# A recurrence in 32 chunks of 32 steps instead of 64 of 16, and an output written in pieces of 2 KB

## The chip, the cores and the metric

The kernel runs on one core of one Trainium2 chip. The metric is the device time of one execution in microseconds (us), taken as the median of several runs; the profile is that of one further execution. A core has a matrix engine (PE, with weight loads listed apart as PEld), a vector engine (DVE), an activation engine (ACT), GpSimd (POOL), SyncE (SP), which here only issues transfers, and 16 DMA engines that all queues share.

## The reference, cut to what matters

Two layers work on x of 8 batches, 1024 tokens (64 by 16) and 128 channels, all float32. Layer 0 is an 8-head attention with two softmaxes and a feed-forward part. Layer 1 adds an additive (tanh) attention and then a recurrent part, and only what follows the recurrent part's input projection is touched here:

```python
Wx = jnp.einsum('bti,hi->bth', x, W)                    # x: layer-normed tokens, 8 x 1024 x 128
Wx = (Wx - mean) * rsqrt(var + 1e-5) * gamma + beta      # mean, var over all 8*1024 tokens
def step(yt, wx_t):
    yt = sigmoid(wx_t + yt @ V.T)
    return (yt, yt)
_, ys = jax.lax.scan(step, zeros, Wx over t)             # 1024 steps, 8 batches side by side
out = t + ys                                             # t: the residual stream
```

The scan has 1024 dependent steps for each batch. V is an orthogonal matrix and the sigmoid's slope is at most a quarter, so that the influence of a state dies away fast: a state that was started from zero some 16 steps too early is, to float32 precision for this purpose, the right one. Both kernels use that.

## The kernel before, in words

The body is `fast_path`. Nearly all of its time is a planned part: `plan.add` collects the operations of both layers for all batches with estimated costs and priorities, and `plan.emit` writes them out in an order of its own. During it, the finished residual stream of each batch goes out to a DRAM buffer `parked[b]` (line 1201, in two transfers of 256 KB), the projected inputs go to `parked_wx[b]`, and near the end they come back into `wx`.

After `main.close()` (line 1318) a straight, hand-ordered stage follows, and this is what the change touches:

- The statistics become a scale `sc` and an offset `off` (lines 1323 to 1330).
- `xr`, the residual stream of all batches, is fetched from `parked` (line 1336, eight transfers of 512 KB).
- DVE writes `ws`, the scaled inputs, one position l of all chunks at a time (line 1342, sixteen instructions of 512 columns).
- The recurrence. The 1024 tokens are cut into NCH = 64 chunks of LCH = 16 steps. All chunks of all batches, 64 x 8 = 512 columns, take one step together. Each chunk first runs through the 16 inputs of the chunk ahead of it (`early`), starting from nothing, and then through its own 16: 32 dependent steps. The 512 columns are two halves of 256 (chunks 0 to 31 and 32 to 63), which take turns. For each half of each step PE adds `ws` through an identity matrix (line 1361) and `V y` (line 1363) in one PSUM bank `acc`, ACT takes the sigmoid into `y` (line 1365), and in the second 16 steps DVE copies `y` to its place in `ys` (line 1370). Float32 matmuls run as two passes each in the trace, so a half step is four passes. The first chunk of a batch has no chunk ahead of it: it is skipped in the early steps, and its state is set to zero by a memset (line 1368).
- The output. For every batch and every four blocks of 128 tokens, PE transposes four blocks of `ys` into a PSUM tile `yt` (line 1378; two tiles), DVE adds `xr` into `ot` (line 1380; three tiles), and a transfer, issued in turn by ACT and SP, writes `ot` to `out` (line 1382). A partition of `ot` holds four tokens that lie 128 tokens apart, so each contiguous piece in DRAM is one token, 512 bytes.

Instructions on one engine run in program order; an engine waits for another only where data or a buffer asks for it.

Of the kernel before, what the change touches and what calls it, by code (L numbers as in the profile page):

```python
# [560 lines left out]
def fast_path(ctx: ExitStack, tc: tile.TileContext, a: dict, fits):  # L561
# [5 lines left out]
    nc = tc.nc  # L567
    NB, N, C = a["x"].shape
    H = a["wqn"].shape[1]
    NT = N // P  # L570
# [1 line left out]
    G = 16  # L572
    M = N // G
    SCALE = 1.0 / math.sqrt(C)
    NCH = 64
    LCH = N // NCH
    NX = 2
    NE = 2
# [3 lines left out]
    dram = ctx.enter_context(tc.tile_pool(name="dram", bufs=1, space=bass.MemoryType.DRAM))  # L582
# [4 lines left out]
    def tile_of(pool, name, shape):  # L587
        return pool.tile(shape, F32, tag=name, name=name)
# [6 lines left out]
    wx = tile_of(keep, "wx", [P, NB, N])  # L595
    parked_wx = [tile_of(dram, f"parked_wx{b}", [P, N]) for b in range(NB - 1)]
    wx_stats = tile_of(keep, "wx_stats", [P, NB, 2, 6])

    parked = [tile_of(dram, f"parked{b}", [P, NT, C]) for b in range(NB)]

    def load(pool, name, shape, eng):
        t = pool.tile(shape, F32, tag=name, name=name + "_sb")
        eng.dma_start(out=t, in_=a[name])
        return t
# [48 lines left out]
    vf_sb = load(const, "vf", [P, C], nc.sync)  # L653
# [8 lines left out]
    ident = tile_of(const, "ident", [P, P])  # L662
# [10 lines left out]
    half = tile_of(const, "half", [P, P])  # L673
# [81 lines left out]
    def through_bank(pe, weight, r, evict, where, more, w, pri, choice=two):  # L755

        bank = Bank(*choice)
        n = len(plan.ops)
        add(("PE", weight), lambda _: pe(bank()), r=r, w=[("bank", n)], pri=pri, take=bank, wait=more + w)
        add(where, lambda e: evict(e, bank()), r=[("bank", n)] + more, w=w, pri=pri, give=bank)  # L760

    def transposes(srcs):
        def fn(bank):
            for i, s in enumerate(srcs):
                nc.tensor.transpose(bank[:, i * P : (i + 1) * P], s, ident)  # L765

        return fn

    def copy(dst):
        def fn(e, bank):  # L770
            src = bank
            if len(dst.shape) == 3:
                src = bank[:, : dst.shape[1] * P].rearrange("p (t c) -> p t c", c=P)
            if e == "ACT":
                nc.scalar.activation(dst, src, AF.Copy)
            else:
                nc.vector.tensor_copy(dst, src)  # L777

        return fn
# [306 lines left out]
    def layer1(b):  # L1086
# [27 lines left out]
        for pair in order:  # L1114
# [48 lines left out]
            for it in range(NT):  # L1163
                if it not in attended and done.issuperset(range(it + 1)):
                    attended.add(it)
                    attention(b, it, X, kX, B, kB, E_at, L1)

    def attention(b, it, X, kX, B, kB, E_at, L1):

        for j0 in range(it + 1, NT, 4):  # L1170
            js = range(j0, min(j0 + 4, NT))
            through_bank(
                transposes([E_sb[:, E_at[it] + j - it, :] for j in js]), 0.08 + 0.12 * len(js),
                [("E", it, j) for j in js],
                copy(ET[:, j0 - 1 : j0 - 1 + len(js), :]), ("DVE", 0.15 + 0.135 * len(js)), [],
                [("ET", j) for j in js], L1,
            )

        def attend(bank):
            for j in range(NT):  # L1180
                lhsT = E_sb[:, E_at[j] + it - j, :] if j <= it else ET[:, j - 1, :]
                nc.tensor.matmul(bank[:, : C + 1], lhsT, B[:, j, :], start=j == 0, stop=j == NT - 1)
# [13 lines left out]
        if it % 4 != 3:  # L1196
            return
        qh = it // 4
        Xg = X[:, 4 * qh : 4 * qh + 4, :]
        add(  # L1200
            ("SP", 4.0), lambda _: nc.sync.dma_start(out=parked[b][:, 4 * qh : 4 * qh + 4, :], in_=Xg),
            r=[kg], w=[("parked", b, qh)], pri=L1,
        )
        layer_norm(Xg, kg, B2, kB2, 4, L1)

        kept = wx[:, b, 512 * qh : 512 * qh + 512] if b == NB - 1 else bT

# [120 lines left out]
    off = rn.tile([P, 1], F32, tag="offb", name="offb")  # L1328
# [1 line left out]
    nc.vector.tensor_tensor(off, beta_sb, off, ALU.subtract)  # L1330


    ys = rn.tile([P, NB, N], F32, tag="ys", name="ys")
    xr = rn.tile([P, NB, NT, C], F32, tag="xr", name="xr")
    for b in range(NB):
        nc.sync.dma_start(out=xr[:, b], in_=parked[b])
    steps = ys.rearrange("p b (c l) -> p c b l", l=LCH)

    ws = rn.tile([P, LCH, NCH, NB], F32, tag="ws", name="ws")
    for l in range(LCH):  # L1340
        step = wx.rearrange("p b (c l) -> p l c b", l=LCH)[:, l]
        nc.vector.tensor_scalar(ws[:, l], step, sc, off, ALU.mult, ALU.add)

    with tc.tile_pool(name="ps_w", bufs=2, space=PSUM) as ps_w, tc.tile_pool(
        name="ps_t", bufs=2, space=PSUM
    ) as ps_t:
        HC = NCH // 2  # L1350
        prev = [None, None]
        for k in range(2 * LCH):
            l = k % LCH
            early = k < LCH
            for half in range(2):
                c0, c1 = half * HC, (half + 1) * HC
                skip = 1 if early and half == 0 else 0
                src = ws[:, l, c0 + skip - early : c1 - early, :]
                acc = ps_w.tile([P, HC, NB], F32, tag=f"acc{half}", name=f"acc{half}")
                to = acc[:, skip:, :]  # L1360
                nc.tensor.matmul(to, ident, src, start=True, stop=k == 0)
                if k:
                    nc.tensor.matmul(to, vf_sb, prev[half][:, skip:, :], start=False, stop=True)
                y = rn.tile([P, HC, NB], F32, tag=f"y{half}", name=f"y{half}", bufs=3)
                nc.scalar.activation(y[:, skip:, :], to, AF.Sigmoid)
                if k == LCH - 1 and half == 0:

                    nc.vector.memset(y[:, 0:1, :], 0.0)
                if not early:
                    nc.vector.tensor_copy(steps[:, c0:c1, :, l], y)  # L1370
                prev[half] = y

        n = 0
        for g in range(NT // 4):
            for b in range(NB):
                pt = ps_t.tile([P, 4, C], F32, tag="yt", name="yt")
                for i in range(4):
                    nc.tensor.transpose(pt[:, i, :], ys[:, b, (4 * g + i) * P : (4 * g + i + 1) * P], ident)
                ot = rn.tile([P, 4, C], F32, tag="ot", name="ot", bufs=3)
                nc.vector.tensor_tensor(ot, pt, xr[:, b, 4 * g : 4 * g + 4, :], ALU.add)  # L1380
                eng = nc.sync if n % 2 else nc.scalar
                eng.dma_start(
                    out=a["out"][b, 4 * g * P : 4 * (g + 1) * P, :].rearrange("(t p) c -> p t c", p=P), in_=ot
                )
                n += 1

# [66 lines left out]
```

## Time and profile before

| | |
|---|---|
| three runs, us | 5839.92, 5830.94, 5828.89; median 5830.94 |
| span of the profiled execution | 5830.7 us |
| PE finishes the last projection of the planned part | 5745.9 us |
| first recurrence matmul starts | 5750.5 us |
| first output transpose starts | 5807.2 us |
| end | 5830.7 us |

The page gives PE 5221.5 us busy (90% of the span), ACT 5291.4 (91%), DVE 4688.8 (80%) and POOL 3850.9 (66%). These are shares over the whole execution, and 98% of it is the planned part. The stage that the change touches is the last 80 us; it has to be read by itself, by giving the queries a window from 5738 us on. There the recurrence takes 5807.2 - 5750.5 = 56.7 us and the output 5830.7 - 5807.2 = 23.5 us. Times in the trace are counted from the start of the span.

### The profile page before, as it was taken

The numbers are of one execution on the slowest core, as the hardware profiler recorded it, in microseconds if no ns is written. First come the engines' busy times: TensorE is split into PE (matmuls) and PEld (weight loads), VectorE is DVE, ScalarE is ACT, GpSimd is POOL, SyncE is SP. The second block draws the span as 40 slices with busy tenths as digits, with TensorE's granted clock in tenths as the row PEclk, the third lists the DMA queues.
The fourth block names the chain that finished last, engine by engine and source line by source line (L and its number), as shares of the span: only waits on it lengthen the run. The fifth ranks groups of instructions, "written<-read, shape, count | busy, mean of one in ns | idle before, by whom it ended". The sixth has DMA issues, their size and how long they took to land.

```text
span 5830.7 us, 96061 instructions
## 1 busy us (share of the span) xinstructions
PE 5221.5 (90%) x38885; PEld 2786.1 (48%) x38885; DVE 4688.8 (80%) x6416; ACT 5291.4 (91%) x5032; POOL 3850.9 (66%) x2414
## 2 busy tenths in 40 slices
PE   9898999899989999899998999989998998987567
PEld 6555544444544455445444444545554444543125
DVE  7989766868897778868889778868798679897885
ACT  5488999999999999889999999999999998999994
POOL 2352698788867897678776887788876876671000
PEclk9999999999999999999999999999999999998999
DMA  2000000000000000000000000000000000000001
GB/s 58 1 4 1 1 1 5 3 6 1 1 5 8 1 1 1 6 6 1 1 5 5 5 1 1 5 8 1 1 1 3 6 1 1 1 21 14 1 1 63
DMA packets 27318, 37.71 MB, mean 6 GB/s; under 512 B 2464, under 2 KB 19232, under 8 KB 26864
## 3 DMA queue, kind: packets, MB, share of 16 engines
q1 hardware_dynamic: 21760, 27.99, 1.4%
q8 instruction: 307, 5.03, 0.4%
q10 hardware_dynamic: 4944, 3.16, 0.2%
q14 instruction: 147, 1.20, 0.1%
q0 software_dynamic: 160, 0.33, 0.0%
HBM read 19.41 MB, written 12.06 MB: 5 GB/s over the span
## 4 chain that ended last, share of the span: by engine, by line
PE 42%; DVE 26%; ACT 25%; issue 5%; POOL 0%; DMA 0%; DVEq 0%; ACTq 0%; POOLq 0%; SPq 0%
PE sa L1053 16%; ACT th L1036 10%; ACT th L993 10%; PE m L899 8%; PE sc L851 7%; PE m L765 4%; DVE th L996 3%; DVE th L1000 3%; DVE stat_e L874 3%; DVE aT L777 3%; DVE stat_e L858 2%; DVE wx L862 2%; ACT sc L854 2%; ACT wx L871 2%; DVE X L737 1%
## 5 line engine op out<-in xcount | busy, mean ns | idle before, releaser
L1000 POOL TENSOR_TENSOR th<-wiT 128x1024 f32<-128x1024 f32 (+58 forms) x1824 | 2795.9, 1565 | 716.0 <-PE sa L1053 674.6
L993 ACT ACTIVATE th<-wiT 128x398 f32<-128x398 f32 (+55 forms) x3180 | 2318.0, 803 | 32.2 <-PE sa L1053 29.2
L1053 PE MATMUL sa<-th,vpat 128*32 128x512 f32 (+29 forms) x24576 | 2113.1, 468 | 250.9 <-ACT th L1036 236.3
L1036 ACT ACTIVATE th<-th 128x3306 f32<-128x3306 f32 (+52 forms) x726 | 1993.6, 2768 | 113.3 <-DVE th L996 73.7
L885 POOL TENSOR_TENSOR wx<-wx,stat_e 128x1024 f32<-128x1024 f32 x512 | 996.0, 1966 | 866.9 <-DVE stat_e L875 663.5
L1053 PEld LDWEIGHTS sa<-th,vpat 128*32 128x32 f32 x24576 | 678.1, 112 | 1512.3 <-issue 834.7
L851 PE MATMUL sc<-xT,wx 128*128 128x512 f32 x2048 | 983.7, 605 | 28.3 <-DVE wx L862 27.8
L899 PE MATMUL m<-aT,wx 128*128 128x256 f32 x3584 | 873.8, 391 | 23.6 <-DVE aT L777 22.4
L899 PEld LDWEIGHTS m<-aT,wx 128*128 128x128 f32 x3584 | 663.2, 192 | 264.9 <-issue 95.3
L777 DVE COPY aT<-m 128x512 f32<-128x512 f32 x925 | 597.1, 673 | 192.6 <-PE m L765 189.9
L858 DVE TENSOR_REDUCE stat_e<-sc 128x16 f32<-128x1024 f32 x512 | 621.1, 1213 | 155.8 <-ACT sc L854 155.0
L996 DVE TENSOR_SCALAR th<-wiT 128x312 f32<-128x312 f32 (+52 forms) x1108 | 655.0, 653 | 64.2 <-PE sa L1053 63.2
L874 DVE TENSOR_REDUCE stat_e<-wx 128x128 f32<-128x2048 f32 x256 | 583.3, 2278 | 108.2 <-ACT wx L871 107.5
L765 PE MATMUL m<-ident,wx 128*128 128x128 f32 x3908 | 574.5, 283 | 89.1 <-DVE aT L777 52.8
L862 DVE TENSOR_TENSOR wx<-sc,stat_e 128x1024 f32<-128x1024 f32 x512 | 624.1, 1219 | 26.0 <-DVE stat_e L859 0.5
L765 PEld LDWEIGHTS m<-ident,wx 128*128 128x128 f32 x3908 | 435.7, 143 | 389.3 <-issue 188.6
L854 ACT ACTIVATE sc<-sc 128x1024 f32<-128x1024 f32 x512 | 513.0, 1005 | 111.5 <-PE sc L851 100.6
L871 ACT ACTIVATE wx<-wx 128x2048 f32<-128x2048 f32 x256 | 486.8, 1901 | 104.9 <-DVE wx L862 104.1
L851 PEld LDWEIGHTS sc<-xT,wx 128*128 128x128 f32 x2048 | 358.6, 193 | 361.3 <-issue 308.0
L1000 DVE TENSOR_TENSOR th<-wiT 128x1024 f32<-128x1024 f32 (+30 forms) x280 | 398.5, 1461 | 5.2 <-PE sa L1053 5.2
L733 POOL TENSOR_TENSOR stat<-stat,neg_half 128x4 f32<-128x4 f32 x64 | 66.5, 1040 | 307.0 <-DVE stat L730 287.7
L875 DVE RECIPROCAL stat_e<-stat_e 128x128 f32<-128x128 f32 x256 | 244.0, 953 | 8.8
(170 smaller groups left out, 2980.6 us busy)
## 6 DMA issues: line engine op xcount, KB each, us to landing
xT<-in_xt_dram SPq DMA_DIRECT2D x8, 512.0 KB, 3.6
th<-in_x_dram SPq DMA_DIRECT2D x8, 512.0 KB, 6.9
parked<-X SPq DMA_DIRECT2D x16, 256.0 KB, 2.0
xr<-parked SPq DMA_DIRECT2D x8, 512.0 KB, 8.2
parked_wx<-bT SPq DMA_DIRECT2D x14, 256.0 KB, 2.0
wx<-parked_wx SPq DMA_DIRECT2D x7, 512.0 KB, 3.3
out_dram<-ot ACTq DMA_DIRECT2D x8, 256.0 KB, 2.5
out_dram<-ot SPq DMA_DIRECT2D x8, 256.0 KB, 2.4
```

The source lines that it names most:

```text
L765: nc.tensor.transpose(bank[:, i * P : (i + 1) * P], s, ident)
L777: nc.vector.tensor_copy(dst, src)
L851: nc.tensor.matmul(sc[:, cols], u[:, qt * P : (qt + 1) * P], xT[:, cols], start=True, stop=True)
L862: nc.vector.tensor_tensor(e3, sc3, r1.unsqueeze(1).to_broadcast([P, M, G]), ALU.mult)
L874: nc.vector.tensor_reduce(r2, e2.rearrange("p q (m g) -> p q m g", g=G), AX.X, ALU.add)
L885: nc.gpsimd.tensor_tensor(e3, e3, r2[:, q, :].unsqueeze(2).to_broadcast([P, M, G]), ALU.mult)
L899: nc.tensor.matmul(bank()[:, :256], vp[:, t, :], aT[:, t, :], start=t == 0, stop=t == NT - 1)
L993: nc.scalar.activation(rows(c)[:, r, :], wiT[:, i0 + begin[c] :], AF.Tanh, bias=w_i(c, r))
L996: nc.vector.tensor_scalar(rows(c)[:, r, :], wiT[:, i0 + begin[c] :], w_i(c, r), None, ALU.add)
L1000: eng.tensor_tensor(rows(c), wiT[:, i0 + begin[c] :].unsqueeze(1).to_broadcast(shape), w_i(c).unsqueeze(2).to_broadcast(shape), ALU.add,)
L1036: lambda _: nc.scalar.activation(slot()[:, : at[4]], slot()[:, : at[4]], AF.Tanh),
L1053: nc.tensor.matmul(sa[32 * c : 32 * c + 32, s:s1], vpat[:, 31 - r0 - r : 63 - r0 - r], rows(c)[:, r, s - at0 - begin[c] : s1 - at0 - begin ...
```

## The change

Three things change together:

- The recurrence runs in NCH = 32 chunks of LCH = 32 steps with 16 early steps (`EARLY`) ahead of them: 48 dependent steps on 32 x 8 = 256 columns. The halves are now four batches each, 128 columns, so that every half has a first chunk to skip in the early steps (124 columns) and to reset. `ws` is made in the order in which the steps need it, in 32 instructions of 256 columns.
- Tokens are dealt to blocks another way. `ys` is laid out so that block t of a batch holds the tokens 8p + t for partition p. A partition of `ot` then holds four neighbouring tokens, 2 KB that are contiguous in `out`. `xr` has to match: `parked[b]` becomes a plain [tokens, channels] buffer, written in 512-byte rows and read back in 4 KB pieces (before: written in 2 KB pieces and read in 4 KB pieces).
- The output loop goes batch by batch, with four `ot` tiles for three and four `yt` tiles in PSUM for two.

It is meant to lower the matrix work of the recurrence and to write the output in larger pieces.

```diff
-    NCH = 64
+    NCH = 32
...
-    parked = [tile_of(dram, f"parked{b}", [P, NT, C]) for b in range(NB)]
+    parked = [tile_of(dram, f"parked{b}", [N, C]) for b in range(NB)]
...
-            ("SP", 4.0), lambda _: nc.sync.dma_start(out=parked[b][:, 4 * qh : 4 * qh + 4, :], in_=Xg),
+            ("SP", 4.0), lambda _: nc.sync.dma_start(
+                out=parked[b][512 * qh : 512 * qh + 512, :].rearrange("(t p) c -> p t c", p=P), in_=Xg
+            ),
...
-        nc.sync.dma_start(out=xr[:, b], in_=parked[b])
-    steps = ys.rearrange("p b (c l) -> p c b l", l=LCH)
+        nc.sync.dma_start(out=xr[:, b], in_=parked[b].rearrange("(p t) c -> p t c", t=NT))
...
+    EARLY = 16
+    HB = NB // 2
+    ws = rn.tile([P, LCH, NB, NCH], F32, tag="ws", name="ws")
+    ys = rn.tile([P, NB, NT, NCH, LCH // NT], F32, tag="ys", name="ys")
+    steps = wx.rearrange("p b (c l) -> p l b c", l=LCH)
+    order = [LCH - EARLY + k for k in range(EARLY)] + list(range(LCH))
+    for l in order[:LCH]:
+        nc.vector.tensor_scalar(ws[:, l], steps[:, l], sc, off, ALU.mult, ALU.add)
...
-        for k in range(2 * LCH):
-            l = k % LCH
-            early = k < LCH
+        for k, l in enumerate(order):
+            early = k < EARLY
+            skip = 1 if early else 0
             for half in range(2):
-                c0, c1 = half * HC, (half + 1) * HC
-                skip = 1 if early and half == 0 else 0
-                src = ws[:, l, c0 + skip - early : c1 - early, :]
-                acc = ps_w.tile([P, HC, NB], F32, tag=f"acc{half}", name=f"acc{half}")
-                to = acc[:, skip:, :]
-                nc.tensor.matmul(to, ident, src, start=True, stop=k == 0)
+                bs = slice(half * HB, (half + 1) * HB)
+                acc = ps_w.tile([P, HB, NCH], F32, tag=f"acc{half}", name=f"acc{half}")
+                to = acc[:, :, skip:]
+                nc.tensor.matmul(to, ident, ws[:, l, bs, 0 : NCH - skip], start=True, stop=k == 0)
...
-                if k == LCH - 1 and half == 0:
+                if k == EARLY - 1:
-                    nc.vector.memset(y[:, 0:1, :], 0.0)
+                    nc.vector.memset(y[:, :, 0:1], 0.0)
                 if not early:
-                    nc.vector.tensor_copy(steps[:, c0:c1, :, l], y)
+                    nc.vector.tensor_copy(ys[:, bs, l % NT, :, l // NT], y)
...
-                    nc.tensor.transpose(pt[:, i, :], ys[:, b, (4 * g + i) * P : (4 * g + i + 1) * P], ident)
-                ot = rn.tile([P, 4, C], F32, tag="ot", name="ot", bufs=3)
+                    t = 4 * g + i
+                    nc.tensor.transpose(pt[:, i, :], ys[:, b, t].rearrange("p c j -> p (c j)"), ident)
+                ot = rn.tile([P, 4, C], F32, tag="ot", name="ot", bufs=4)
                 nc.vector.tensor_tensor(ot, pt, xr[:, b, 4 * g : 4 * g + 4, :], ALU.add)
                 eng = nc.sync if n % 2 else nc.scalar
                 eng.dma_start(
-                    out=a["out"][b, 4 * g * P : 4 * (g + 1) * P, :].rearrange("(t p) c -> p t c", p=P), in_=ot
+                    out=a["out"][b].rearrange("(p t) c -> p t c", t=NT)[:, 4 * g : 4 * g + 4, :], in_=ot
                 )
```

More of the change, by code (lines that the diff above doesn't have):

```diff
@@ L1330, in fast_path @@
     nc.vector.tensor_tensor(off, beta_sb, off, ALU.subtract)
-    ys = rn.tile([P, NB, N], F32, tag="ys", name="ys")
     xr = rn.tile([P, NB, NT, C], F32, tag="xr", name="xr")
     for b in range(NB):
-        nc.sync.dma_start(out=xr[:, b], in_=parked[b])
-    steps = ys.rearrange("p b (c l) -> p c b l", l=LCH)
[L1339 to L1342, printed above, removed]
+        nc.sync.dma_start(out=xr[:, b], in_=parked[b].rearrange("(p t) c -> p t c", t=NT))
@@ L1347, in fast_path @@
+    EARLY = 16
[6 more added lines that the diff above has]
+        nc.vector.tensor_scalar(ws[:, l], steps[:, l], sc, off, ALU.mult, ALU.add)
     with tc.tile_pool(name="ps_w", bufs=2, space=PSUM) as ps_w, tc.tile_pool(
-        name="ps_t", bufs=2, space=PSUM
+        name="ps_t", bufs=4, space=PSUM
@@ L1349, in fast_path @@
     ) as ps_t:
-        HC = NCH // 2
         prev = [None, None]
-        for k in range(2 * LCH):
-            l = k % LCH
-            early = k < LCH
+        for k, l in enumerate(order):
+            early = k < EARLY
+            skip = 1 if early else 0
             for half in range(2):
-                c0, c1 = half * HC, (half + 1) * HC
-                skip = 1 if early and half == 0 else 0
-                src = ws[:, l, c0 + skip - early : c1 - early, :]
-                acc = ps_w.tile([P, HC, NB], F32, tag=f"acc{half}", name=f"acc{half}")
-                to = acc[:, skip:, :]
-                nc.tensor.matmul(to, ident, src, start=True, stop=k == 0)
-                if k:
-                    nc.tensor.matmul(to, vf_sb, prev[half][:, skip:, :], start=False, stop=True)
-                y = rn.tile([P, HC, NB], F32, tag=f"y{half}", name=f"y{half}", bufs=3)
-                nc.scalar.activation(y[:, skip:, :], to, AF.Sigmoid)
-                if k == LCH - 1 and half == 0:
-                    nc.vector.memset(y[:, 0:1, :], 0.0)
+                bs = slice(half * HB, (half + 1) * HB)
+                acc = ps_w.tile([P, HB, NCH], F32, tag=f"acc{half}", name=f"acc{half}")
+                to = acc[:, :, skip:]
+                nc.tensor.matmul(to, ident, ws[:, l, bs, 0 : NCH - skip], start=True, stop=k == 0)
+                if k:
+                    nc.tensor.matmul(to, vf_sb, prev[half][:, :, skip:], start=False, stop=True)
+                y = rn.tile([P, HB, NCH], F32, tag=f"y{half}", name=f"y{half}", bufs=3)
+                nc.scalar.activation(y[:, :, skip:], to, AF.Sigmoid)
+                if k == EARLY - 1:
+                    nc.vector.memset(y[:, :, 0:1], 0.0)
@@ L1369, in fast_path @@
                 if not early:
-                    nc.vector.tensor_copy(steps[:, c0:c1, :, l], y)
+                    nc.vector.tensor_copy(ys[:, bs, l % NT, :, l // NT], y)
                 prev[half] = y
         n = 0
-        for g in range(NT // 4):
-            for b in range(NB):
+        for b in range(NB):
+            for g in range(2):
                 pt = ps_t.tile([P, 4, C], F32, tag="yt", name="yt")
                 for i in range(4):
-                    nc.tensor.transpose(pt[:, i, :], ys[:, b, (4 * g + i) * P : (4 * g + i + 1) * P], ident)
-                ot = rn.tile([P, 4, C], F32, tag="ot", name="ot", bufs=3)
+                    t = 4 * g + i
+                    nc.tensor.transpose(pt[:, i, :], ys[:, b, t].rearrange("p c j -> p (c j)"), ident)
+                ot = rn.tile([P, 4, C], F32, tag="ot", name="ot", bufs=4)
```

## The prediction

> **What bounds it now.** I read the page first, but its shares (PE 90%, ACT 91%) are those of the planned part, which both kernels share instruction for instruction: the order of instructions on each engine differs only after it, and in the shape of the `parked` transfers. So I cut the tail into stages, by the table of busy time per window (columns: length, then busy time and instructions of PE, PEld, DVE, ACT, POOL, the granted PE clock, the DMA share and GB/s):
>
> ```profile
> 5750.40:5755.40 5.00, 4.93 (x12) 4.06 (x13) 5.00 (x8) 2.30 (x4) 0.00 (x0) 0.50 0.98 383
> 5755.40:5778.90 23.50, 23.50 (x112) 21.03 (x111) 5.28 (x9) 10.48 (x29) 0.00 (x0) 1.00 0.13 51
> 5778.90:5807.20 28.30, 28.25 (x131) 24.51 (x130) 13.11 (x31) 12.44 (x34) 0.00 (x0) 1.00 0.00 1
> 5807.20:5825.20 18.00, 11.33 (x64) 7.82 (x64) 11.18 (x17) 0.37 (x1) 0.00 (x0) 0.91 0.72 204
> ```
>
> In the recurrence PE has no gap at all (23.50 of 23.50, 28.25 of 28.30) while ACT and DVE are half idle or more. It is bound by PE passes, not by the dependence of one step on the next. In the output (last row) nothing is full: PE 11.3 of 18.0, DVE 11.2, DMA 0.72. That points to a ring of buffers. The timeline of PE and ACT in one step, then of two earlier stretches of 128 columns:
>
> ```profile
> 5780.22 0.59 PE L1361 MATMUL acc<-ws,ident 128*128 128x256 f32 x2
> 5780.65 0.59 PE L1363 MATMUL acc<-y,vf_sb 128*128 128x256 f32 x2
> 5781.08 0.59 PE L1361 MATMUL acc<-ws,ident 128*128 128x256 f32 x2
> 5781.52 0.59 PE L1363 MATMUL acc<-y,vf_sb 128*128 128x256 f32 x2
> ...
> 5781.28 0.38 ACT L1365 ACTIVATE y<-acc 128x256 f32<-128x256 f32 x1 [0.48 <-PE acc L1363]
> ...
> 5735.95 1.95 PE L1182 MATMUL m<-B,E 128*128 128x129 f32 x16
> ```
>
> A pair of passes starts every 0.43 us: a pass of 256 columns costs 0.216 us, a step (8 passes) 1.73 us. The L1182 row prices what the change will run: 16 passes of 129 columns with their weight loads in 1.95 us, the last one's own length some 0.28, so (1.95 - 0.28) / 15 = 0.111 us a pass. The waits from 5807 us on show the ring of the output:
>
> ```profile
> PEld yt L1378 <- DVE ot L1380: 8.8, 13, 1.4
> DVE ot L1380 <- DMA out_dram<-ot: 4.8, 10, 1.1
> ```
>
> PE waits for DVE to free `yt`, and DVE waits, in 10 of 16 groups, for a transfer to free one of three `ot` tiles. The end of the chain hangs on the transfers.
>
> **What the Trainium skill says.** "TensorE: Matmul & The Clock Gate", under LDWEIGHTS, prices a weight load by its columns over 1.2 GHz: 107 ns for 128, an estimate that fits the 0.111 us above; so at 128 columns a pass cannot become cheaper than its weight load. The same page, under "What's actually happening", says that PE runs at half clock after an idle window of about 3.4 us and at full clock after a busy one, in free-running windows. The trace agrees: clock 0.50 from 5741.8 to 5755.5 us, then 1.00. Going through the trace in such windows, those that lifted the clock had PE busy 77% or more, and those that lost it 50% or less. "ScalarE: Activation LUTs", "What ACT_TABLE_LOAD costs", gives 0.83 ns per column; the trace has 383 ns at 256 columns and 1005 at 1024 (line 854), 0.81 ns. So a sigmoid of 128 columns takes 383 - 128 x 0.81 = 279 ns. "DMA: Bandwidth & Descriptors" gives 512 bytes as enough for line rate in its table of specifications; this trace does not agree: the output's 4.19 MB in 512-byte pieces kept the two queues at 31.0 and 30.9% of 24 us, that is 14.9 us of all 16 engines (280 GB/s), while a 256 KB transfer in 2 KB pieces (`parked`, 5738 to 5742 us) moved at 389 to 410 GB/s.
>
> **The change, part by part.**
>
> (1) Recurrence. The passes fall from 32 x 8 of 256 columns to 48 x 8 of 128. A step costs PE 8 x 0.110 = 0.88 us. For that to hold, `y` of one half must be ready when its turn comes, 0.88 us later. The chain: weights and two passes of V (0.11 + 0.11 + 0.27 for the last one's length) 0.49, PE's end to ACT's start 0.04 (5781.24 to 5781.28), sigmoid 0.28, ACT's end to PE 0.05 (as from DVE's copy to the first transpose, 5807.15 to 5807.20): 0.86 us. It fits by 0.02. That is my least safe term; if it doesn't fit, the excess of the chain is paid in every step. I bound the step by 0.87 (weight loads alone) and 1.0 (a wait that also lays a weight load bare), and take 0.88.
>
> Start: the first `ws` instruction has 256 columns for 512, 0.27 us shorter; the first accumulation ends some 0.4 sooner at half clock. The sigmoid's table load (1.28 us, from 5751.7) follows it, and so comes 0.67 us sooner; the first sigmoid is 0.1 shorter, and PE does fewer passes in between. The first V pass goes from 5753.54 to about 5752.65. From there 47 steps x 0.88 = 41.4 us. The half clock costs half of the time that it lasts after 5752.65. If the window from 5752.05 to 5755.46 still counts as busy (I put PE at some 80% there, on the edge of 77), 1.4 us, else until 5758.9, 3.1 us: 2.2 taken. One pair of passes is done ahead (-0.2). First transpose at 5752.65 + 41.4 + 2.2 - 0.2 = 5796.0, for 5807.2: **11.2 us less**. The same sum for before, 5753.54 + 31 x 1.72 + 1.0 - 0.9, gives 5807.0.
>
> Beside it: DVE makes `ws` in 32 instructions of about 0.43 us (the 512-column ones start every 0.69; 256 columns less is 0.27), one per step of 0.88, so it stays ahead. It is done by 5763.5, before the two memsets queued behind it, which the 17th step waits for (about 5767). DVE's 64 copies at 0.34 or less (128x128 tensor_scalar of line 737: 342 ns) and ACT's 96 sigmoids at 0.28 fill 0.68 and 0.56 us of each 0.88, nobody's bound.
>
> (2) Output. Before, a group took (5824.45 - 5807.90) / 15 = 1.103 us, so a turn of three `ot` tiles 3.31 us: add, issue, landing, next add. With four tiles and the same turn 0.83. The pieces of 2 KB shorten the transfer itself from 14.9 / 16 = 0.93 to 256 KB / 385 GB/s = 0.68 us, so a turn of 3.06 and 0.77. The floors are 0.68 by DMA and 0.61 by DVE (5807.90 to 5808.51). I take 0.75, kept between 0.68 and 0.83. PE needs 4 x 0.11 = 0.44 a group and has four tiles. Stage: 0.70 to the first add + 15 x 0.75 + 0.69 + 5.56 of tail (last add's end 5825.14 to 5830.7, last landing and shutdown; kept) = 18.2 us for 23.5: **5.3 us less**.
>
> (3) `parked` in 512-byte rows: 16 transfers of 0.93 for 0.68 us, all but the last far ahead of their use. The last one landed by 5740.5, and the fetch of `xr` waits until 5746.0 for PE's last projection, so 0.25 us more is hidden. `xr` (still 4 KB pieces, done by 5758) is first needed at 5796: nothing.
>
> Sum: -11.2 - 5.3 = -16.5 us; 5830.9 - 16.5 = **5814.4**, say 5814.5.
>
> **Rivals.** (a) *The chain binds*: 128 columns leave no slack, and a step takes 1.0 us. 47 x 0.12 = +5.6: 5820, in the range of no change. For it: 0.02 us of slack. Against it: a late `y` only moves the turn, and a weight load that waits alone is followed by its pass after half its length in the transposes' records. (b) *The output stays on its ring*: small pieces were not the limit, landing time is, 1.0 us a group: +3.8, 5818. (c) *PE loses its clock*: waits in every step let the clock fall to half, and a step costs 8 x 0.216 = 1.73 us for the whole recurrence: 47 x 0.85 = +40 less the 2.2 counted, about 5852, **slower**. Against it: busy shares stay over 80% even at 1.0 us a step, and only 50% or less lost the clock. (d) *All goes well*: clock lifted at 5755.5, 0.68 a group: -0.8 - 1.05, 5812.6.
>
> **Chances.** Main 0.58, (d) 0.12, (b) 0.10: all faster. (a) 0.12: no change. (c), with anything that the different DRAM writes might do to the planned part, 0.05: slower. The last 0.03, and the spread of the three runs (11 us), I divide: faster 0.80, same 0.14, slower 0.06. The range goes from 5806 (the floors, 5812, and a low set of runs) to 5822 (case a and a little more).
>
> **What would show it.** Right: `acc` passes every 0.11 us and steps of 0.88 with PE without gaps; first transpose near 5796; groups of 0.75 us; the same planned part up to 5750. Wrong: ACT and PE waiting for each other in each step (a); DVE waiting for transfers at 1 us a group (b); clock 0.50 past 5760 (c).

## The result and the profile after

The changed kernel takes **5816.64 us** (median of 20 runs, 5808.59 to 5835.78); the kernel before 5838.43 us (20 runs, 5826.66 to 5850.50). The ratio over all runs is **0.997, with a 95% interval of 0.9961 to 0.9979**. Of 5838 us that is 17.5 us less, between 12 and 23; the prediction took off 16.5. The ratio is close to that of the means (5820.35 and 5838.03 us); the two medians lie 21.8 us apart.

The two profiled executions seem to contradict this: 5829.8 us after, 5830.7 before. The planned part, the same in both, ended at 5745.9 us in the profile of before and at 5761.9 in that of after. In the profiles of the kernels below, which all share it, PE's last projection ends anywhere from 5742.6 to 5773.1 us. So I count each stage from the end of that projection (the last `m<-bT,wf_sb` matmul), and use single totals for nothing.

| from the last projection's end, us | before | predicted | after |
|---|---|---|---|
| first V pass | 8.03 (7.6 for its weights) | 6.75 | 6.73 |
| clock at full | 9.52 | 9.5 to 13 | 9.65 |
| first output transpose | 61.27 | 50.1 | 49.75 |
| end | 84.81 | 68.3 | 67.95 |
| the output stage alone | 23.54 | 18.2 | 18.20 |
| a group of the output | 1.103 | 0.75 | 0.724 |
| a step of the recurrence | 1.73 | 0.88 | 0.893 |

The busy time per window of after, with the same columns as in the prediction (length; busy time of PE, PEld, DVE, ACT, POOL; granted clock; DMA share; GB/s), for the start at half clock, the recurrence twice, and the output:

```profile
5766.20:5771.50 5.30, 4.89 (x21) 4.60 (x22) 5.30 (x14) 2.55 (x6) 0.00 (x0) 0.50 1.00 397
5771.50:5785.00 13.50, 13.50 (x123) 13.50 (x122) 8.89 (x24) 8.25 (x30) 0.00 (x0) 1.00 0.20 78
5785.00:5811.60 26.60, 26.60 (x241) 26.60 (x240) 16.80 (x60) 16.57 (x60) 0.00 (x0) 1.00 0.01 2
5811.60:5824.00 12.40, 9.07 (x66) 6.78 (x65) 10.96 (x18) 0.36 (x2) 0.00 (x0) 1.00 0.79 293
```

PE still has no gap in the recurrence, and now neither has PEld: a weight load lies under every pass (26.60 of 26.60 us). The timeline of after follows one half through a step:

```profile
5789.98 0.39 PE L1365 MATMUL acc<-y,vf_sb 128*128 128x128 f32 x2
...
5790.41 0.28 ACT L1367 ACTIVATE y<-acc 128x128 f32<-128x128 f32 x1 [0.17 <-PE acc L1365]
...
5790.77 0.30 PEld L1365 LDWEIGHTS acc<-y,vf_sb 128*128 128x128 f32 x2
...
5790.88 0.39 PE L1365 MATMUL acc<-y,vf_sb 128*128 128x128 f32 x2
```

V's passes end at 5790.37, the sigmoid runs from 5790.41 to 5790.69, and the half's next V starts its weight load at 5790.77. This is the first instruction that has to wait for `y`. With 0.05 us from ACT to PE, `y` is 0.03 us early. Eight passes in 0.893 us make 0.1117 us a pass.

In the output, the views of waits and of groups of instructions seem to say that DVE is the bound now:

```profile
DVE ot L1383 <- DMA out_dram<-ot: 0.8, 2, 0.5
...
L1383 DVE TENSOR_TENSOR ot<-yt,xr 128x512 f32<-128x512 f32 x16 | 10.5, 689 | 1.0 <-DMA out_dram<-ot 0.8 <-PE yt L1381 0.2
```

DVE waited in 10 of 16 groups for a transfer, 4.8 us in all; now twice, for 0.8 us, and an add takes 689 ns of the 724 between groups. The timeline of DVE in the output shows that this reading is wrong:

```profile
5812.30 2.48 DVE L1383 TENSOR_TENSOR ot<-yt,xr 128x512 f32<-128x512 f32 x4
5815.27 2.67 DVE L1383 TENSOR_TENSOR ot<-yt,xr 128x512 f32<-128x512 f32 x4 [0.49 <-DMA out_dram<-ot]
5818.20 2.71 DVE L1383 TENSOR_TENSOR ot<-yt,xr 128x512 f32<-128x512 f32 x4 [0.26 <-DMA out_dram<-ot]
5821.09 2.77 DVE L1383 TENSOR_TENSOR ot<-yt,xr 128x512 f32<-128x512 f32 x4 [0.18 <-PE yt L1381]
```

The first four adds, which find their tiles free, start every 0.60 us: (2.48 - 0.68) / 3. So the records of two adds overlap by 0.08 us, and a wait of up to that length leaves no idle time between records. From the fifth add on, every add starts 0.12 us (the fifth 0.19) after the landing of the transfer that held its tile, four groups earlier; the transfers of the first two groups land at 5815.08 and 5815.77, and the fifth and sixth adds start at 5815.27 and 5815.89. The output still hangs on its ring of tiles, with a shorter turn: an add of 0.69, 0.03 to the transfer's issue, 2.1 from there to its landing, and 0.12 to the next add make 2.94 us, over four tiles 0.73. The 2.1 us are those of the view of transfers:

```profile
out_dram<-ot ACTq DMA_DIRECT2D x8, 256.0 KB, 2.1
```

The transfers themselves are not far from full: 0.96 of the DMA engines' time from 5815.3 to 5821.1 us.

### The profile page after: what moved, and what is told of

It reads as the page before. It is cut to its first block, busy times and chain, and to the rows that moved or that the text cites. A ratio compares the mean times of both kernels' runs of the same rounds, so it can differ in the third digit from the quotient of the medians.

```text
span 5829.8 us, 96427 instructions
## 1 busy us (share of the span) xinstructions
PE 5209.0 (89%) x39013; PEld 2778.0 (48%) x39013; DVE 4713.6 (81%) x6465; ACT 5294.0 (91%) x5064; POOL 3853.2 (66%) x2414
## 4 chain that ended last, share of the span: by engine, by line
PE 42%; DVE 27%; ACT 25%; issue 5%; POOL 0%; DMA 0%; DVEq 0%; ACTq 0%; POOLq 0%; SPq 0%
PE sa L1053 16%; ACT th L1036 10%; ACT th L993 10%; PE m L899 8%; PE sc L851 7%; PE m L765 4%; DVE th L1000 3%; DVE th L996 3%; DVE aT L777 3%; DVE stat_e L874 3%; DVE stat_e L858 2%; DVE wx L862 2%; ACT sc L854 2%; ACT wx L871 2%; DVE X L737 1%
```

## The experiments

All stages are counted from the last projection. "First transpose" and "end" are times after it. Each row is one profile. In the last three rows the first transposes already stand inside the recurrence, so that their "group" averages over two stages.

| kernel | first V | clock full | step | first transpose | group | output stage | end |
|---|---|---|---|---|---|---|---|
| before | 8.03 | 9.52 | 1.73 | 61.27 | 1.103 | 23.54 | 84.81 |
| changed | 6.73 | 9.65 | 0.893 | 49.75 | 0.724 | 18.20 | 67.95 |
| e1_pieces512 | 6.72 | 11.30 | 0.893 | 50.53 | 0.907 | 21.01 | 71.54 |
| e2_ring32 | 6.73 | 11.31 | 0.893 | 50.54 | 0.957 | 21.49 | 72.03 |
| e3_rec_only | 6.73 | 9.27 | 0.893 | 49.57 | 1.155 | 24.17 | 73.74 |
| e4_one_half | 6.90 | 56.99 | 1.160 | 54.21 | - | - | 79.65 |
| e5_loose | 6.72 | 8.79 | 0.893 | 49.34 | 0.723 | 17.68 | 67.02 |
| e8_half_filled | 8.08 | 7.90 | 0.855 | 43.48 | - | - | 65.25 |
| e6_start | 5.53 | 5.41 | 0.893 | 47.30 | 0.724 | 17.86 | 65.16 |
| e7_best | 5.53 | 5.41 | 0.893 | 45.29 | 0.721 | 18.38 | 63.67 |
| e9_best2 | 5.15 | 4.46 | 0.893 | 45.19 | 0.721 | 18.47 | 63.66 |
| e11_best3 | 5.17 | 4.50 | 0.893 | 40.78 | 0.721 | 18.38 | 59.16 |

### The output: pieces, ring, and neither

My theory: the pieces shorten a turn of the ring, and the number of tiles divides it. Rival: one of the two does all of it. The number of `yt` tiles was changed together with that of `ot` tiles, not alone. The three kernels are the changed one with (1) 512-byte pieces, (2) rings of three `ot` and two `yt`, (3) both.

```diff
# e1 (and e3)
-                    t = 4 * g + i
+                    t = 2 * i + g
-                nc.vector.tensor_tensor(ot, pt, xr[:, b, 4 * g : 4 * g + 4, :], ALU.add)
+                nc.vector.tensor_tensor(ot, pt, xr[:, b, g::2, :], ALU.add)
-                    out=a["out"][b].rearrange("(p t) c -> p t c", t=NT)[:, 4 * g : 4 * g + 4, :], in_=ot
+                    out=a["out"][b].rearrange("(p t) c -> p t c", t=NT)[:, g::2, :], in_=ot
# e2 (and e3)
-        name="ps_t", bufs=4, space=PSUM
+        name="ps_t", bufs=2, space=PSUM
-                ot = rn.tile([P, 4, C], F32, tag="ot", name="ot", bufs=4)
+                ot = rn.tile([P, 4, C], F32, tag="ot", name="ot", bufs=3)
```

> The changed kernel with the tokens of a partition taken in every second place, so that the output goes out in pieces of 512 bytes again; four ot and four yt tiles stay. Recurrence as in the changed kernel (steps of 0.89 us). Theory 'both': data time of a 256 KB transfer is back at 14.9/16 = 0.93 us, which is above a quarter of the old turn (3.31/4 = 0.83), so groups come every 0.93 us and the stretch from the first transpose to the end is 0.7 + 15 x 0.93 + 0.7 + 5.9 = 21.2 us (18.2 in the changed kernel, 23.5 before). Rival 'ring alone': the size of pieces did nothing, 0.72 us a group, 18.2 us. Rival 'pieces alone': back to 1.10 us a group, 23.5 us.

> The changed kernel with three ot tiles and two yt tiles as before; pieces of 2 KB stay. Theory 'both': a turn of three tiles costs 3.31 - 0.24 = 3.07 us, 1.02 us a group, first transpose to end 0.7 + 15 x 1.02 + 0.7 + 5.9 = 22.6 us. Rival 'pieces alone': 0.72 us a group, 18.2 us. Rival 'ring alone': 1.10 us a group, 23.5 us.

> The changed recurrence with the output of before: three ot tiles, two yt tiles, pieces of 512 bytes. All theories of the output: 1.10 us a group and 23.5 us from the first transpose to the end, as before. The stretch from the end of PE's last projection to the first transpose as in the changed kernel, 49.7 us (61.3 before). If the gain of the recurrence depended on the output part, it would not be 49.7.

Measured: groups of 0.907, 0.957 and 1.155 us, against 0.724. A turn of the ring (group by number of `ot` tiles) is 4 x 0.907 = 3.63 and 3 x 1.155 = 3.46 us with 512-byte pieces, 3 x 0.957 = 2.87 and 4 x 0.724 = 2.90 with 2 KB. The groups of e1 and e2 were expected at 0.93 and 1.02 us: e1 came out close, e2 turned faster than expected. With three tiles the pieces alone take 3.46 - 2.87 = 0.59 us off a turn. Almost all of it lies between issue and landing: the median there is 2.6 us in e3 and 2.05 in e2, and in both every add from the fourth on starts 0.12 to 0.19 us after a landing. So the theory holds in both halves: the pieces shorten the turn, and the tiles divide it. The two effects add up: 0.20 and 0.25 us a group for either alone, 0.43 for both. The waits of e1 in its output (us in all, times, longest) have DVE waiting for a transfer in 12 of 16 groups:

```profile
DVE ot L1383 <- DMA out_dram<-ot: 3.5, 12, 1.1
```

The same line in the waits of e2:

```profile
DVE ot L1383 <- DMA out_dram<-ot: 2.5, 6, 0.7
```

And in those of e3, with neither, where the total is the largest (waits shorter than the overlap of two adds are missing from all three):

```profile
DVE ot L1383 <- DMA out_dram<-ot: 6.8, 12, 1.4
```

With 512-byte pieces and four tiles the transfers are full: the DMA engines moved 269 to 317 GB/s in every slice of that output after the one in which it began, and 262 KB at 0.907 us is 289 GB/s. There the pieces are the bound; with 2 KB and three tiles it is the ring, since the rate falls to 29 and 15 GB/s between transfers that reach 380 to 400. The recurrence alone (e3) brings the first transpose from 61.27 to 49.57, 11.7 us; the output part brings 24.17 - 18.20 = 6.0 us to that. The output of e3 was expected at the 23.54 us of before and took 24.17. Its 512-byte pieces lie 1 KB apart in `out`, those of before side by side from partition to partition; whether that is the cause was not tried. Counted from the output of before, the output part brings 5.3 us.

### The recurrence: passes or chain

My theory: passes bind, by a hair. Rival (a) of the prediction: the chain binds. Three kernels take them apart. `e5_loose` lets V read the state of two steps back, so its results are those of another recurrence, and the chain has twice the time:

```diff
-                    nc.tensor.matmul(to, vf_sb, prev[half][:, :, skip:], start=False, stop=True)
+                    nc.tensor.matmul(to, vf_sb, prev[half][max(k - 2, 0)][:, :, skip:], start=False, stop=True)
-                y = rn.tile([P, HB, NCH], F32, tag=f"y{half}", name=f"y{half}", bufs=3)
+                y = rn.tile([P, HB, NCH], F32, tag=f"y{half}", name=f"y{half}", bufs=4)
-                if k == EARLY - 1:
+                if k in (EARLY - 2, EARLY - 1):
-                prev[half] = y
+                prev[half].append(y)
```

> The changed kernel with V applied to the state of two steps back: the true dependence of a step on the one before is left out, the number of passes, sigmoids and copies stays. Theory 'passes bind': nothing changes, a step stays at 0.893 us and the first transpose 49.6 to 50.5 us after the last projection. Rival 'chain binds': with a whole step of slack PE runs at its bare pass time, 8 x 0.107 = 0.86 us a step, 1.5 us less in all.

Measured: 0.893 us a step, no change. A chain that binds would have given something back.

`e4_one_half` computes only the first four batches (and copies their states to the places of the others), to lay the chain bare:

```diff
-            for half in range(2):
+            for half in range(1):
```

> Only the first half (four batches) of the recurrence is computed; its states are copied to the places of the other half, so that batches 5 to 8 of the output are left out. PE has 4 passes a step (0.45 us) and the rest of each step is the bare dependence of a step on the one before. Theory 'passes bind': the chain alone is shorter than the step of 0.893 us in the changed kernel, 0.80 to 0.86 us. Rival 'chain binds': what I took for passes is the chain, and a step stays at 0.89 us or more although half of the passes are gone.

Measured: 1.160 us a step, but not the chain that I was after. The windows of this kernel show why:

```profile
5760.00:5770.00 10.00, 10.00 (x36) 8.20 (x36) 3.72 (x10) 2.19 (x8) 0.00 (x0) 0.50 0.00 0
5770.00:5790.00 20.00, 20.00 (x71) 15.89 (x69) 6.68 (x32) 4.93 (x18) 0.00 (x0) 0.50 0.00 1
```

The clock stays at 0.50 for the whole recurrence. A pass at half clock starts every 0.215 us (in e7_best below, pairs follow each other by 0.43), so four passes fill 0.86 of 1.16 us, 74%. The PE column says 10.00 of 10.00 all the same, since the records of PE there, 0.79 and 0.64 us for the two pairs of a step, together are longer than the step and also cover time in which no pass runs. This is rival (c) of the prediction, real when PE is fed too little.

So `e8_half_filled` computes one half again, but keeps the other half's identity passes, whose results nobody reads, as a filling of six passes a step:

```diff
-                nc.tensor.matmul(to, ident, ws[:, l, bs, 0 : NCH - skip], start=True, stop=k == 0)
+                nc.tensor.matmul(to, ident, ws[:, l, bs, 0 : NCH - skip], start=True, stop=k == 0 or half == 1)
+                if half:
+                    continue
```

> As the kernel with one half alone (batches 5 to 8 of the output left out), but PE keeps the other half's two ws passes, which nobody reads, so that it has 6 passes a step (0.67 us) and should get its full clock back: at half clock they fill 6 x 0.213 = 1.28 us, more than the 1.16 us of the chain at half clock that the half alone showed. Theory 'passes bind': at full clock the step is the bare chain, 0.80 to 0.86 us, shorter than 0.893. Rival 'chain binds': 0.89 us or more. If the clock stays at half: 1.28 us.

Measured: the filling runs ahead at the start and lifts the clock 7.90 us after the projection, where it stays, and a step takes 0.855 us, with six passes of 0.112 = 0.67 us in it. Its timeline:

```profile
5785.55 0.49 PE L1367 MATMUL acc<-y,vf_sb 128*128 128x128 f32 x2
...
5786.07 0.28 ACT L1369 ACTIVATE y<-acc 128x128 f32<-128x128 f32 x1 [0.58 <-PE acc L1367]
...
5786.40 0.30 PEld L1367 LDWEIGHTS acc<-y,vf_sb 128*128 128x128 f32 x2 [0.16 <-ACT y L1369]
```

V's passes, with the wait for their weights, end at 5786.04; the sigmoid takes 5786.07 to 5786.35; the next weight load starts at 5786.40 and is marked as waiting for `y`. That is the bare chain: **0.855 us against 0.893 us of passes**. The passes bind, by 0.04 us.

### The rows of `parked`

The kernel before with this part alone:

```diff
-    parked = [tile_of(dram, f"parked{b}", [P, NT, C]) for b in range(NB)]
+    parked = [tile_of(dram, f"parked{b}", [N, C]) for b in range(NB)]
-            ("SP", 4.0), lambda _: nc.sync.dma_start(out=parked[b][:, 4 * qh : 4 * qh + 4, :], in_=Xg),
+            ("SP", 4.0), lambda _: nc.sync.dma_start(
+                out=parked[b][512 * qh : 512 * qh + 512, :].rearrange("(t p) c -> p t c", p=P), in_=Xg),
-        nc.sync.dma_start(out=xr[:, b], in_=parked[b])
+        nc.sync.dma_start(out=xr[:, b], in_=parked[b].rearrange("(t p) c -> p t c", p=P))
```

> The kernel before with one part of the change alone: parked[b] is a [tokens, channels] buffer, written in 512-byte rows (and, since its blocks keep their tokens, read back into xr in 512-byte pieces too, which lands a few us later and is not needed until the output). If the prediction's 'nothing' for this part holds, the time is that of the kernel before: ratio 1.000 (0.999 to 1.001), and from the last projection to the end 84.8 us. Rival: the writes hold up the planned part, or the longer fetch of xr holds up the output; then the ratio is 1.001 or more, and as much of the gain of the other parts was lost in the changed kernel. If the rows helped, below 0.999.

Measured: ratio 1.0008, interval 0.9996 to 1.0021 (14 runs against 19); the last stage took 85.26 us for 84.81, with steps and groups alike. No gain and no loss that this can tell. In the last stage the longer fetch of `xr` (here in 512-byte pieces, in the changed kernel in 4 KB) costs nothing. A loss of up to 12 us in the planned part, where the writes are, isn't excluded: the interval allows it, and the part's own spread hides it in single profiles.

### What is left: the start, the early steps, the output under the recurrence

The changed kernel starts its recurrence at half clock and with a sigmoid table load in its chain. `e6_start` loads the table during the statistics and lets PE run six identity matmuls that nobody reads while it waits for them:

```diff
+    warm = rn.tile([P, 1], F32, tag="warm", name="warm")
+    nc.vector.memset(warm, 0.0)
+    nc.scalar.activation(warm, warm, AF.Sigmoid)
...
+        for _ in range(2):
+            pt = ps_t.tile([P, 4, C], F32, tag="yt", name="yt")
+            for i in range(3):
+                nc.tensor.matmul(pt[:, i, :], ident, ident, start=True, stop=True)
```

> The changed kernel with the sigmoid's table loaded ahead (a sigmoid of one column right after the planned part) and six matmuls on the identity that nobody reads, before the first accumulation, to bring the clock back sooner. Theory of the start: the first V pass comes 1.28 us sooner, at 5.45 us after the last projection (6.73 in the changed kernel); the clock lifts 1.5 to 4 us sooner than 9.3 to 11.3, which is worth half of that; first transpose at 46.8 to 48.0 us after the last projection (49.6 to 50.5). Rival: the idle PE's clock doesn't care for a few passes, or the passes delay the start: only the table's 1.28 us or less, 48.3 or more.

Measured: the first V pass at 5.53 us (6.73), the clock lifted at 5.41, ahead of it (9.65), and the first transpose at 47.30, for 49.75. The four profiles with this start have the lift at 4.5 to 5.4 us, the six with the start of the changed kernel at 8.8 to 11.3. The two parts were not tried one by one; the 1.2 us of the first V pass are near the table load's 1.28. The windows of this kernel, the lift at 5751.1:

```profile
5743.60:5751.10 7.50, 6.03 (x20) 4.37 (x21) 4.29 (x13) 1.77 (x4) 0.55 (x1) 0.50 0.54 196
5751.10:5755.00 3.90, 3.90 (x37) 3.90 (x37) 3.90 (x9) 2.46 (x9) 0.00 (x0) 1.00 1.02 400
```

`e7_best` adds to this 12 early steps for 16 (a quarter to the twelfth power is 6e-8, so a false start still dies away) and writes the first half of each batch's output during the last four steps, with six `ot` tiles:

```diff
-    EARLY = 16
+    EARLY = 12
...
+        def write(b, g, n):
+            ...
+            ot = rn.tile([P, 4, C], F32, tag="ot", name="ot", bufs=6)
...
+            if not early and l >= 28:
+                for b in (2 * (l - 28), 2 * (l - 28) + 1):
+                    write(b, 0, b)
...
         for b in range(NB):
-            for g in range(2):
+            write(b, 1, b)
```

> The start as in the kernel before this one; 12 early steps for 16 (four steps of 0.893 us less); six ot tiles; the first half of each batch's output (tokens 8p to 8p+3) goes out during the last four steps, two groups a step, since it needs no state after step 27. From the end of the last projection to the end of the span: 67.95 us in the changed kernel, less 2.4 (start), 3.6 (steps) and about 2.8 (output begun earlier, 0.68 us a group): 59.2 us. In all some 25 us under the kernel before, ratio about 0.9956; the changed kernel gave 0.997. If the output's groups in the last steps hold up PE for what they save later: 61.5 us.

Measured: the end at 63.67 us, a miss by over 4. Ratio to the kernel before 0.9961 (0.9945 to 0.9977). The timeline of PE in this kernel, with a standstill ahead of its second row:

```profile
5760.30 0.39 PE L1382 MATMUL acc<-ws,ident 128*128 128x128 f32 x2
5763.07 0.46 PE L1384 MATMUL acc<-y,vf_sb 128*128 128x128 f32 x2 [2.39 <-DVE y L1389]
...
5764.71 0.64 PE L1384 MATMUL acc<-y,vf_sb 128*128 128x128 f32 x2
5765.14 0.63 PE L1382 MATMUL acc<-ws,ident 128*128 128x128 f32 x2
```

The timeline of DVE in it:

```profile
5759.76 3.15 DVE L1354 TENSOR_SCALAR ws<-wx,scb,offb 128x256 f32<-128x256 f32 x7
5762.85 0.07 DVE L1389 MEMSET y<- 128x4 f32 x2
```

Memsets of 0.07 us stand in DVE's queue behind all 32 `ws` instructions. With four early steps fewer and an earlier start, PE needs them before DVE gets there, and stands still for 2.4 us. And then the pairs of passes start 0.43 us apart, not 0.22: the clock fell to half from 5764.2 to 5767.6, which costs half of 3.4, 1.7 us. The wait that the prediction found hidden at 16 early steps (3.5 us to spare by its sum, 3.7 in the trace) binds at 12.

`e9_best2` moves the memsets to GpSimd (`nc.gpsimd.memset` for `nc.vector.memset`).

> As the kernel before this one, with the two memsets on GpSimd, which is idle here, for DVE. There PE stood still for 2.5 us at the end of the early steps: the memsets waited behind DVE's 32 ws instructions, the window's busy share fell and the clock went to half for 3.4 us. Theory 'memset's queue': stall and half clock go away, 2.5 + 1.7 us less, from the end of the last projection to the end of the span 63.7 - 4.2 = 59.5 us. In all about 25 us under the kernel before (ratio 0.9957) and 8 under the changed kernel. Rival: DVE's queue hits again elsewhere (the copies of the first own steps wait behind ws, the ring of three y fills), 61 us or more.

Measured: 63.66 us; ratio 0.9958 (0.9946 to 0.9971). A miss again. The timeline of POOL:

```profile
5756.99 4.87 POOL L1389 MEMSET y<- 128x4 f32 x2 [9.96 <-PE acc L1384]
```

The timeline of PEld, at the load that waits for it:

```profile
5761.90 0.30 PEld L1384 LDWEIGHTS acc<-y,vf_sb 128*128 128x128 f32 x2 [2.71 <-POOL y L1389]
```

The two memsets of four columns are under way for 4.87 us on GpSimd, until 5761.86; DVE's unbroken run of `ws` ended at 5761.80. The Trainium skill, "SBUF — State Buffer", under "SBUF: two separate sides", says that DVE and GpSimd share a port pair by an exclusive lock, and that the loser "fully blocks". The two ends 0.06 us apart fit that, but only in part: the page has the lock held for one instruction, and by DVE only in certain modes, and here the memsets waited through some eleven instructions of DVE. No run takes the lock apart from another cause. In any case the work left DVE's queue and did not get out of DVE's way.

`e11_best3` does it by order: the two tiles whose columns are cleared have buffers of their own, and DVE clears them before its first `ws` instruction.

```diff
+    yz = [rn.tile([P, HB, NCH], F32, tag=f"yz{half}", name=f"yz{half}") for half in range(2)]
+    for half in range(2):
+        nc.vector.memset(yz[half][:, :, 0:1], 0.0)
     for l in order[:LCH]:
         nc.vector.tensor_scalar(ws[:, l], steps[:, l], sc, off, ALU.mult, ALU.add)
...
                 if k == EARLY - 1:
-                    nc.vector.memset(y[:, :, 0:1], 0.0)
+                    y = yz[half]
+                else:
+                    y = rn.tile([P, HB, NCH], F32, tag=f"y{half}", name=f"y{half}", bufs=3)
```

> As e7_best, with the two columns that the memsets clear taken in tiles of their own and cleared on VectorE ahead of its 32 ws instructions. If the memsets behind ws were what held TensorE for 2.5 us and cost 1.7 us more at half clock, both go: from the end of the last projection to the end 63.7 - 2.5 - 1.7 = 59.5 us (59 to 61), first V pass as in e6_start (about 5.2 to 5.6 us after the projection), no stretch at clock 0.50 after the lift, and the time some 8 us under the changed kernel, 0.995 to 0.9957 of the kernel before. Rival: VectorE's queue holds elsewhere behind ws (the first copies of the steps, or the ring of y), so that a stall of over 1 us stays: 61 us or more.

Measured: **59.16 us**, as expected. Its windows, the recurrence from the lift of the clock on and then the output:

```profile
5748.10:5760.00 11.90, 11.90 (x106) 11.80 (x106) 11.90 (x28) 7.06 (x26) 0.00 (x0) 1.00 0.67 262
5760.00:5784.40 24.40, 24.40 (x221) 24.40 (x221) 16.22 (x60) 15.22 (x55) 0.00 (x0) 1.00 0.01 2
5784.40:5797.00 12.60, 10.45 (x90) 9.50 (x88) 11.38 (x24) 1.74 (x8) 0.00 (x0) 1.00 0.76 279
```

No gap, no half clock. DVE's timeline at the end of its output, and the window around it:

```profile
5791.06 5.46 DVE L1367 TENSOR_TENSOR ot<-yt,xr 128x512 f32<-128x512 f32 x9
```

```profile
5791.00:5797.00 6.00, 3.85 (x30) 2.90 (x28) 5.53 (x11) 0.00 (x0) 0.00 (x0) 1.00 0.98 365
```

With six tiles the ring no longer binds: tiles come free 0.66 us or more before their adds, and nine adds start every 0.60 us, (5.46 - 0.68) / 8. That is DVE's own pace. Now the transfers are full (0.98), and from issue to landing they take 2.1 us for the first of these groups and 2.6 toward the end (the last three apart, which land over 4 us after their issue). The 0.721 us of the table is no pace: it averages these 0.60 us with the wider spacing of the groups written during the last steps. By the trace this is 8.8 us shorter than the changed kernel's stage. The time is 5810.68 us (17 runs, against 5834.20 of before in 21): ratio 0.9963, 0.9955 to 0.9972, a little less gain than the 0.995 to 0.9957 expected. Beside e9_best2 the changed kernel was run once more.

> The changed kernel once more, beside the best version, for a comparison on one chip: 67.0 to 69.6 us from the end of the last projection to the end of the span, ratio to the kernel before 0.997.

Measured: 5815.15 us, ratio 0.9971 (0.9962 to 0.9981), and an end 68.68 us after the projection. The intervals of the two overlap, so these totals don't separate the last version from the changed kernel; the stages in the trace do, since there the planned part's spread is taken out, and the two profiles of the changed kernel differ by 0.7 us.

## Why the prediction came out right, point by point

- **The recurrence is bound by PE's passes (part 1): right.** A pass takes 0.1117 us for 0.110 predicted, a step 0.893 for 0.88, within the bounds of 0.87 and 1.0. Making the chain looser changed nothing, and the bare chain is 0.855 us, for an estimate of 0.86. So the slack is 0.04 us; the estimate of 0.02 came from a pass that was 0.0017 us too short. The 0.111 us that the prediction had read from its L1182 row would have given 0.89; it went on with 0.110. Its lower bound of 0.87 for weight loads alone is 8 x 0.107 = 0.86. Whether a pass of 128 columns is held by its weight load or by its columns, no run here takes apart.
- **The start: right.** First V pass 6.73 us after the projection (6.75 predicted), as the table load moved forward. `ws` was done at 5779.6, 17.7 us after the projection (17.6 predicted); no wait at the memsets.
- **The clock: right within its choice, and by luck in part.** The half clock lasted 2.9 us after the first V pass and cost half of that, 1.5, the lower of the two values between which I took 2.2. In other profiles of kernels with the same start the lift came at 8.8 to 11.3 us instead of 9.65: its phase moves from execution to execution, and with it up to 1.3 us.
- **First transpose: -11.5 us for -11.2.** Steps that were 0.6 us longer in all (47 x 0.013) and a clock that cost 0.7 less made up for each other; with the lift at 11.3 us (e10) the first transpose came at 50.53, 0.4 us later than predicted.
- **The output: right in both causes, and the 18.20 us partly by luck.** The prediction had a turn of 3.06 us over four tiles; it is about 2.94, since the pieces took some 0.4 to 0.6 us off it (against before and against e3) where 0.25 was put. The groups are thus 0.4 us shorter in all (15 x 0.026) than predicted, and the tail after the last add is 6.0 us for 5.56, which cancels that. The floors, 0.68 by DMA and 0.61 by DVE, were not reached with four tiles. The 0.61 is right for DVE: 0.60 wherever adds follow each other freely.
- **`parked` (part 3): nothing, as predicted,** as far as 1.0008 (0.9996 to 1.0021) tells.
- **The rivals.** The group of 0.724 and the early lift lie towards (d), which would have given 2 us less still. (a) fell with e5 and e8. (b) was right that the output stays on its ring, and wrong about the turn: 1.0 us a group needs one of 4 us. But for the pieces, or but for the ring, it would have come nearly true (0.907 and 0.957). (c) didn't happen, with eight passes a step. But my argument against it was bad: I took "busy 77%" from records, and records that show PE busy all the time (e4) went with a clock that never rose. What counts there seems nearer to passes times their pitch; no run here finds the share that lifts or keeps the clock.
- **The total: nearer than it had a right to be.** 5814.4 us was counted from 5830.94, the median of three runs of before; its twenty runs have 5838.43. With that base the same sum gives 5821.9, for 5816.64 measured. The gain itself, 16.5 us, is borne out by the stages: 84.81 - 67.95 = 16.9 us, and 16.1 with e10.

## What to carry to other kernels

When a recurrence takes turns on PE, work out both the sum of passes and the bare chain for one step; the larger binds. Here the cut of the columns brought the two to where they nearly meet (0.893 and 0.855 us); no other cut was tried. For a ring of output tiles, measure one turn, divide by the tiles, and compare with the floors of every engine that serves it: pieces and tiles both helped, and four tiles still bound (0.72 us a group, for floors of 0.68 by DMA and 0.60 by DVE). Take the pace of an engine from the starts of instructions that follow each other freely, not from their mean length, and a wait from the landing it hangs on: here records of 0.69 us hid waits, and a ring looked like a busy engine. A short instruction behind a long stream on its engine is free only while its consumer comes late: after every speed-up look again at what is queued ahead of it.

## What the runs showed of the hardware

- With passes filling about 74% of the time at half clock (e4), PE's clock did not rise once in the 47 us of the recurrence, though the records show PE busy throughout. In e8 a run of 18 identity passes without a wait, from 5746.87 to 5750.5, lifted it at 5750.5, and six passes a step (0.67 of 0.855 us, 78% of the time at full clock) then kept it.
- A standstill of 2.4 us in a full recurrence (e7) cost its own length and 1.7 us more, by one stretch of 3.4 us at half clock; without it (e11) the stage is 4.5 us shorter, of which 0.4 us is an earlier first V pass.
- Two GpSimd memsets of 128x4 beside a stream of DVE instructions took 4.9 and 4.4 us, both until that stream ended (e9); on DVE one takes 62 ns (e7).
- A DVE add of 128x512 float32, one operand in PSUM, has a record of 0.68 to 0.69 us, but adds that follow each other freely start every 0.60 us (after, e11).
- From issue to landing, a 256 KB transfer to `out` took 2.05 us in pieces of 2 KB (e2) and 2.6 in pieces of 512 bytes (e3), with at most three under way.
- The last add's end to the end of the execution took 5.3 to 6.3 us in all of these kernels, whatever the ring; nothing in the change touches it.
